# Neighbour rows of layer 0 summed by accumulating gathers, with running sums of ranks in columns beside each row

## The chip, the core and the metric

The kernel runs on one core of one Trainium2 chip. The engines are named as in the profile: PE (TensorE, matrix products), DVE (VectorE), ACT (ScalarE), POOL (GpSimd) and SP (SyncE, which here only issues DMA transfers). POOL issues the indirect transfers: gathers and scatters of rows by a list of indices. The metric is the device time of one execution in microseconds (us).

## What is computed

The reference takes node features `x` (3327 x 512, float32), a sparse random adjacency matrix `adj` (3327 x 3327, integers, about 0.12% ones) and the weights of four graph layers. Each layer adds its result to `x`:

```python
h = maximum(layernorm(x), 0)
# layer 0
mask = (adj > 0); deg = sum(mask, axis=1)
agg = mask @ h / maximum(deg, 1)
out = concat([h @ W_self + b_self, agg @ W_nb + b_nb]) @ W_comb + b_comb
x = x + relu(out)
# layers 1 to 3: graph attention with 8, 4 and 1 heads
e = leaky_relu(f_src[i] + f_dst[j], 0.2), only where adj > 0
x = x + softmax(e) @ (h @ W)      # layer 2 with an elu around the result
```

The result is the `x` after layer 3.

## The kernel before

**Two paths in one program.** `gnn_stack_kernel` holds a fast path, which uses lists of neighbours, and at its end a branch. The one-element tile `flag_i` says whether the fast path was allowed to do what it did; if it is not zero, `general_path` (from L26) computes all four layers again with the dense adjacency matrix and writes the output anew.

```python
    general = nc.values_load(
        flag_i[0:1, 0:1], min_val=0, max_val=1, skip_runtime_bounds_check_because="the result of a comparison"
    )
    with tc.If(general != 0):
        general_path(
```

**Chunks and slots.** Nodes are kept in chunks of 128 (NK = 26 chunks, D = 512 columns). The fast path reads `adj` once, finds the neighbours of each node and sorts the nodes by degree, so that chunk 0 holds the nodes of highest degree. `ROWS` (L564) says how many nodes, at most, have more than 0, 1, 2, ... neighbours: 3328, 3072, 2592, 1984, ... down to 32, 32, 32, 32, 0, 0. From it follows how many neighbour slots a chunk has: 14 for chunk 0, 8 for chunk 1, then fewer, and 1 for chunks 24 and 25, in all 117. SLOTS is 16.

**The first stage** (L852 to L1513) fuses the weights of layer 0, multiplies each chunk by both fused matrices (`pz` for the neighbours' part, `py` for the node's own), stores the neighbours' part into a table in device memory (`table[0]`) and reads `adj`. Then the nodes are sorted: `places` (L1415) works in the tile `work`, 416 columns (W = SLOTS x NK) at a time. Columns 0 to 415 take `run`, the running counts of nodes by degree class, and columns 416 to 831 take `place`; out of these come `rank`, the position of each node, and its integer form. `spread` (L1461) copies the ranks into a tile `rank4` of 4 columns per node, which `store_rank` writes beside each row of `table[0]`, so that a gathered row brings along the position of its node. `scatter` moves each node's record to its sorted position in `own`.

**The flag.** `certain` (L1472) adds up three kinds of doubt: whether the neighbour lists agree with the row's sum of squares, whether a node has more than 16 neighbours, and whether a degree class has more nodes than `ROWS` allows. The last reads `run` at the end of each class, every 26th column from 25, and compares it with `caps`, which holds `ROWS` from its end, so from 0, 0, 32 up to 3328:

```python
                    nc.vector.tensor_tensor(
                        over, box["run"].rearrange("p (d k) -> p d k", k=NK)[:, :, NK - 1], caps, ALU.is_gt
                    )
```

`tell` sums the doubts of all partitions by a matmul (L1492), and `flag` (L1496) makes `flag_i` of whether the sum is above zero.

**Layer 0 and the attentions** (from L1516). `gather` (L1545) issues one indirect transfer per slot, each of up to 128 rows, into the next free places of a ring of 33 rows (`ring`). In layer 0 the index comes from the node's record (`srec`), in layers 1 to 3 from `nbr`, the positions that layer 0 has taken from the gathered rows (L1862). In layer 0, PE adds up the first slots by multiplying with the identity (`sum_on_pe`, L1593), DVE scales that sum by 1/degree and adds the node's own part (L1871) and the bias (L1879), adds the remaining slots, scaled, one by one (L1887), and adds relu of that to x (L1895). `project` (L1602) then normalises the chunk, turns it (L1694), multiplies it with the weights of the next layer (L1780) and stores the rows of the next table. `attend` (L1911) does an attention layer over the same slots.

**The order** is not that of the source. Each stage hands its steps to a `Plan` (L614), with an engine, an estimated cost, a rank and what they wait for. `Plan.run` walks through them by these costs and emits them in the order of their planned starts; each engine then keeps that order. `ORDERS` (L578) gives the order of the chunks by layer, in units of one or two chunks. A layer's first gather waits until all rows of its table are stored (the `mark` at L2194).

**The general path** has no slots. Layer 0 (L136 to L251) projects all chunks, then reads `adj` by chunk, clips it (L213), makes a row code of it (L214), turns it on PE (L223), multiplies the turned mask with the projected rows (L232) and stores the codes (L227, L228, L235 to L237). `attention` (L254) runs once for each of layers 1 to 3: projections of all chunks (L291 to L309), the maximum over each row's neighbours, by head, with one DVE instruction over 1664 columns in layers 1 and 2 and 3328 in layer 3 (L351, after L347 in layer 3), and then, by block of four chunks, head and chunk, the scores and their product with the values:

```python
                                nc.scalar.activation(
                                    t2[:, :w], sb[:, 1, :w], AF.Identity, bias=fd02[:, k, h : h + 1]
                                )
                                nc.vector.scalar_tensor_tensor(
                                    v[:, kk, :w], sb[:, 0, :w], fsd[:, k, d : d + 1], t2[:, :w], ALU.add, ALU.max
                                )
```

These are L419 and L422; L426 adds the mask, L429 takes the exponential, and PE multiplies at L434 (layer 1), L446 (layer 2) or L439 and L442 (layer 3).

Of the kernel before, what the change touches and what calls it, by code (L numbers as in the profile page):

```python
# [8 lines left out]
F32 = mybir.dt.float32  # L9
# [9 lines left out]
P = 128  # L19
# [7 lines left out]
def general_path(  # L27
# [519 lines left out]
    def l3_finish(pc, i, o):  # L547
# [24 lines left out]
ON_DVE = {  # L572
    0: {S: min(S // 2, 5) for S in range(1, SLOTS + 1)},
    1: {S: min(S // 2, 5) for S in range(1, SLOTS + 1)},
    2: {S: 0 for S in range(1, SLOTS + 1)},
}

ORDERS = {  # L578
    0: (
        (24,), (12, 21), (11,), (6,), (18,), (17,), (15,), (4,), (3,), (20,), (5, 9), (22,), (10, 19), (1,),  # L580
        (2,), (14,), (0,), (23,), (8,), (13, 16), (7,), (25,),
    ),
# [110 lines left out]
def gnn_stack_kernel(  # L693
# [32 lines left out]
    heads = {1: l1_w.shape[0], 2: l2_w.shape[0], 3: 1}  # L726
    width = {0: D + 4, 1: D + 8, 2: D + 4, 3: D + 4}
    WIDE = D + 8

# [5 lines left out]
    with ExitStack() as st:  # L735
# [116 lines left out]
        with tc.tile_pool(name="p0", bufs=1) as pa, tc.tile_pool(name="p0p", bufs=2, space=PSUM) as pp:  # L852
# [312 lines left out]
            def empty_rows():  # L1165
                nc.gpsimd.memset(null, 0.0)
                nc.gpsimd.tensor_copy(null[:, 0, D:], null_f[:, 0:1].to_broadcast([P, WIDE - D]))
                nc.gpsimd.memset(null[:, 1, D:], NEVER)
# [128 lines left out]
            for p0 in range(0, NK, 2):  # L1297
# [25 lines left out]
                for j, i in enumerate(unit):  # L1323
# [136 lines left out]
            with nc.allow_non_contiguous_dma(reason="each node's record and place beside its row"):  # L1460
                def spread():  # L1461
                    rank4 = pa.tile([P, NK, 4], F32, tag="rank4", name="rank4")
                    nc.vector.tensor_copy(rank4, box["rank"].unsqueeze(2).to_broadcast([P, NK, 4]))
# [52 lines left out]
        with tc.tile_pool(name="run", bufs=1, reuse_waits="tile") as pr, tc.tile_pool(  # L1516
# [28 lines left out]
            def gather(layer, i, rank, barrier):  # L1545
# [8 lines left out]
                for s in range(S):  # L1554
# [291 lines left out]
            for number, unit in enumerate(ORDERS[0]):  # L1846
                rank = (0, number)
                updated = []
                for j, i in enumerate(unit):
# [14 lines left out]
                    last.append(plan.add("dve", 0.03 + 0.17 * len(runs_of(i, 0, S)), rank, emit, landed))  # L1864
                    left = S - ON_DVE[0][S]
                    summed = sum_on_pe(key, g, list(range(left)), [[o] for o in landed], rank)
                    last += summed

                    def emit(i=i, key=key):
                        acc = tiles["acc", key]  # L1870
# [4 lines left out]
                    done = plan.add("dve", 0.7, rank, emit, [summed[-1], own_in])  # L1875

                    def emit(key=key):
                        acc = tiles["acc", key]
                        nc.vector.tensor_tensor(acc, acc, biasf, ALU.add)  # L1879

                    done = plan.add("dve", 0.7, rank, emit, [done])
                    for s in range(left, S):

                        def emit(i=i, key=key, g=g, s=s):
                            m = held(i, s)
                            acc = tiles["acc", key][:m, :]
# [4 lines left out]
                        done = plan.add("dve", 0.7, rank, emit, [done, landed[s]])  # L1891
                        last.append(done)

# [17 lines left out]
            def attend(layer, number, unit, barrier):  # L1911
# [348 lines left out]
```

## Time and profile before

| what | us |
|---|---|
| median of 14 runs | 1075.08 (1071.61 to 1080.6) |
| the profiled execution | 1075.53 |
| its span, first to last instruction | 1073.6 |

The mean granted clock of PE in this execution was 0.899 of full speed. By stage, busy us of each engine (from a question on five stretches of the span):

| stretch, us | stage | PE | DVE | ACT | POOL | granted clock | DMA share |
|---|---|---|---|---|---|---|---|
| 0 to 266 | adjacency, sorting, first products | 231.78 | 187.30 | 163.20 | 104.96 | 0.96 | 0.87 |
| 266 to 449 | layer 0 | 167.20 | 130.62 | 78.60 | 110.22 | 0.98 | 0.81 |
| 449 to 620 | layer 1 | 143.06 | 144.44 | 103.01 | 129.83 | 0.92 | 0.73 |
| 620 to 870 | layer 2 | 200.23 | 171.52 | 125.76 | 140.46 | 0.82 | 0.53 |
| 870 to 1073 | layer 3 | 134.37 | 91.62 | 47.54 | 135.12 | 0.83 | 0.62 |

How to read the lines that follow. A line of the timeline has the start in us from the span's start, the duration in us, the engine, the line of the source, the operation, what it writes and reads (written as out<-in), the shape, and the count where equal ones are merged; in brackets the idle time before it and what ended that. A line of a group has the same names, the count, and after the bar the busy time in us, the mean duration of one in ns, and the idle time before them. A float32 matmul appears as two PE records where it multiplies, and as one where it turns a tile. "DMA share" is the mean busy share of the core's 16 DMA engines.

### The profile page before, as it was taken

To read this page: it belongs to the slowest core of one execution; us is meant where nothing else is said; L and a number is where in the kernel's file an instruction comes from. 1 tells how busy PE (TensorE), PEld (TensorE's weight loads), DVE (VectorE), ACT (ScalarE), POOL (GpSimd) and SP (SyncE) were. 2 spreads that over 40 slices of the span, in tenths; PEclk is the share of its full clock that TensorE was granted. 3 is DMA by queue.
4 is the path that set the end of the run, shared out by engine and by line. 5 is a ranking of instruction groups with operands and counts; after the bars stand their busy time and mean duration, and the time that the engine had idled before them with its cause. 6 is when DMAs were issued, how large, how long until landed. Compare 5 with 4: busy or idle time off the path is not lost. (4 is left out here: it accounts for less than half of the span.)

```text
span 1073.6 us, 11605 instructions
## 1 busy us (share of the span) xinstructions
PE 876.6 (82%) x2853; PEld 499.2 (46%) x2853; DVE 725.5 (68%) x1848; ACT 518.1 (48%) x1700; POOL 620.6 (58%) x719
## 2 busy tenths in 40 slices
PE   7699999994899998569998983897989814949785
PEld 4244444441476665446665652444544412424332
DVE  6499989920787769278998882787885808435541
ACT  3398887631353534346677641564663612214221
POOL 1051444673777772277787604788777057777671
PEclk9899999997899999879999987798878956979887
DMA  9999888399999986277777604767766147677671
GB/s 350 313 371 392 308 300 302 125 310 327 298 331 311 339 280 195 92 202 219 235 209 216 186 22 125 203 192 204 219 184 173 57 126 190 200 206 208 189 200 54
DMA packets 89910, 240.49 MB, mean 224 GB/s; under 512 B 24933, under 2 KB 26477, under 8 KB 89834
## 3 DMA queue, kind: packets, MB, share of 16 engines
q0 software_dynamic: 41600, 137.72, 43.9%
q1 hardware_dynamic: 48234, 101.96, 26.8%
q8 instruction: 24, 0.39, 0.1%
q14 instruction: 52, 0.43, 0.1%
HBM read 190.35 MB, written 49.27 MB: 223 GB/s over the span
## 5 line engine op out<-in xcount | busy, mean ns | idle before, releaser
L1562 POOL DMA_INDIRECT ring<-table,nbr x351 | 379.0, 1080 | 117.1 <-issue 64.4
L1593 PE MATMUL acc<-ring,ident 128*128 128x512 f32 (+1 forms) x494 | 257.5, 656 | 71.7 <-DVE ring L2110 46.0
L1780 PE MATMUL pw<-w,hT 128*128 128x264 f32 (+1 forms) x832 | 194.3, 390 | 2.8 <-ACT hT L1705 2.8
L1780 PEld LDWEIGHTS pw<-w,hT 128*128 128x128 f32 x832 | 160.1, 193 | 43.5 <-ACT hT L1705 9.7
L1593 PEld LDWEIGHTS acc<-ring,ident 128*128 128x128 f32 (+1 forms) x494 | 95.6, 208 | 175.8 <-issue 79.0
L1562 POOL DMA_INDIRECT ring<-table,srec x117 | 110.2, 942 | 45.5 <-issue 20.1
L2110 DVE TENSOR_TENSOR ring<-ring,w 128x2048 f32<-128x2048 f32 (+7 forms) x76 | 114.3, 1532 | 1.8
L1941 DVE TENSOR_TENSOR e<-ring,fs 128x24 f32<-128x24 f32 (+25 forms) x96 | 15.3, 172 | 132.7 <-DMA ring<-table,nbr 129.0
L1209 DVE FIND_INDEX8 fidx<-one_i,ai 128x8 uint32<-128x832 int32 x104 | 104.2, 1018 | 0.0
L2060 PE MATMUL pw<-w,hT 128*128 128x512 f32 x208 | 98.9, 620 | 5.8 <-ACT hT L2052 5.8
L1217 ACT ACTIVATE junk<-ai 128x1664 int8<-128x1664 int32 (+1 forms) x52 | 82.8, 1591 | 30.1 <-DMA ai<-in_adj_dram 29.6
L1349 PE MATMUL pz_n<-wf,hT_n 128*128 128x512 f32 x208 | 92.3, 595 | 0.9 <-ACT hT_n L1342 0.8
L1349 PE MATMUL py_n<-wf,hT_n 128*128 128x512 f32 x208 | 91.9, 592 | 0.0
L1705 ACT ACTIVATE hT<-pt 128x128 f32<-128x128 f32 (+1 forms) x312 | 81.7, 292 | 21.1 <-PE pt L1694 20.7
L2060 PEld LDWEIGHTS pw<-w,hT 128*128 128x128 f32 x208 | 41.1, 201 | 61.8 <-issue 46.8
L1705 ACT ACTIVATION_READ_ACCUMULATOR hT<-pt 128x1 f32 x312 | 69.4, 223 | 0.0
L822 ACT ACTIVATE ln<-mv,eps 128x1 f32<-128x1 f32 (+1 forms) x60 | 18.0, 300 | 96.2 <-DVE mv L1650 87.7
L1968 ACT ACTIVATE ex<-el 128x48 f32<-128x48 f32 (+19 forms) x56 | 12.8, 232 | 104.3 <-DVE el L1951 104.3
L1349 PEld LDWEIGHTS pz_n<-wf,hT_n 128*128 128x128 f32 x208 | 39.0, 190 | 50.5 <-issue 45.2
L2046 PE MATMUL pt<-ident,y 128*128 128x128 f32 x96 | 15.6, 294 | 56.4 <-DVE y L2030 51.0
L2194 POOL MEMSET mark<- 1x1 f32 x3 | 0.3, 88 | 106.0 <-DMA table<-t 106.0
L2030 DVE SCALAR_TENSOR_TENSOR acc<-ring,w,acc 128x512 f32<-128x512 f32 (+2 forms) x67 | 50.5, 754 | 13.6 <-ACT acc L2028 12.0
(185 smaller groups left out, 1321.8 us busy)
## 6 DMA issues: line engine op xcount, KB each, us to landing
ai<-in_adj_dram SPq DMA_DIRECT2D x25, 832.0 KB, 7.2
ai<-in_adj_dram SPq DMA_DIRECT2D x25, 831.5 KB, 7.3
table<-t SPq DMA_DIRECT2D x52, 258.0 KB, 3.4
xy<-own SPq DMA_DIRECT2D x26, 512.0 KB, 5.6
table<-t SPq DMA_DIRECT2D x26, 260.0 KB, 5.4
table<-zt_n SPq DMA_DIRECT2D x26, 256.0 KB, 5.9
ring<-table,nbr POOLq DMA_INDIRECT x351, 3.8
later<-in_x_dram SPq DMA_DIRECT2D x15, 256.0 KB, 6.7
```

What stands on the lines that cost most here:

```text
L822: nc.scalar.activation(ln, var, AF.Ln, bias=eps, scale=scale)
L1209: nc.vector.max_index(fidx[:, i, qq * 8 : (qq + 1) * 8], one_i, ai[:, q * QW : min(cols, (q + 1) * QW)])
L1217: nc.scalar.activation(junk[:, :cols], tiles["ai", key][:, :cols], AF.Square, accum_out=sq[:, i, hf : hf + 1])
L1349: nc.tensor.matmul(pz, tiles["hT", key][:, c, :], wf[s][:, c, :], start=(c == 0), stop=(c == DC - 1))
L1562: nc.gpsimd.indirect_dma_start(out=ring[:m, r0 + s, : width[layer]], out_offset=None, in_=table[layer], in_offset=bass.IndirectOffsetOnAxi ...
L1593: nc.tensor.matmul(acc, ident[:m, :], g[:m, s, :D], start=(k == 0), stop=(k == len(slots) - 1))
L1705: nc.scalar.activation(hT[:, c, :n], pt[:, c, :n], AF.Copy, accum_out=hsum[layer][:, i, c : c + 1])
L1780: nc.tensor.matmul(pw[:, b, :w], tiles["hT", key][:, c, :], wsb[layer][:, c, b, :w], start=(c == 0), stop=(c == DC - 1),)
L2030: nc.vector.scalar_tensor_tensor(to[:m, :], row, weight, acc[:m, :], ALU.mult, ALU.add)
L2046: nc.tensor.transpose(pt[:, c, :], tiles["y", key][:, c * P : (c + 1) * P], ident)
L2060: nc.tensor.matmul(pw[:, 0, :], tiles["hT", key][:, c, :], w3[:, c, :], start=False, stop=(c == DC - 1))
L2110: nc.vector.tensor_tensor(v, v, box["w"][:m, j, lo:hi, :].unsqueeze(3).to_broadcast([m, hi - lo, H, O]), ALU.mult,)
```

## The change

In layer 0 each chunk now takes one row of the ring instead of one per slot. The first slot is gathered into it, and every further slot is gathered on top with an adding transfer. The ranks move ahead of the row and take 16 columns instead of 4; a chunk with S slots gathers slot s from column 16 - S + s on, so that rank column 16 - S + s takes the ranks of slots 0 to s. The positions are then the first of these columns and the differences of neighbouring ones. ACT scales the sum by 1/degree into PSUM, and DVE adds the own part and the bias. The copy of the ranks goes into columns of the tile `work` instead of a tile of its own. The order of chunks in layer 0 is another, and `AHEAD` sets how much earlier than its chunk each slot's transfer is ranked.

```diff
 ON_DVE = {
-    0: {S: min(S // 2, 5) for S in range(1, SLOTS + 1)},
...
+AHEAD = 0.9
...
     0: (
-        (24,), (12, 21), (11,), (6,), (18,), (17,), (15,), (4,), (3,), (20,), (5, 9), (22,), (10, 19), (1,),
-        (2,), (14,), (0,), (23,), (8,), (13, 16), (7,), (25,),
+        (23,), (22,), (17, 18), (21,), (24,), (9,), (13,), (19,), (11,), (3,), (16,), (5,), (4,), (12,), (6, 20), (2,),
+        (14,), (8,), (15,), (7,), (10,), (1,), (0,), (25,),
...
-    width = {0: D + 4, 1: D + 8, 2: D + 4, 3: D + 4}
-    WIDE = D + 8
+    width = {0: D + SLOTS, 1: D + 8, 2: D + 4, 3: D + 4}
+    WIDE = D + SLOTS
...
-                nc.gpsimd.tensor_copy(null[:, 0, D:], null_f[:, 0:1].to_broadcast([P, WIDE - D]))
+                nc.gpsimd.tensor_copy(null[:, 0, :SLOTS], null_f[:, 0:1].to_broadcast([P, SLOTS]))
...
-                        nc.sync.dma_start(table[0][i * P : (i + 1) * P, :D], tiles["zt", key])
+                        nc.sync.dma_start(table[0][i * P : (i + 1) * P, SLOTS:], tiles["zt", key])
...
                 def spread():
-                    rank4 = pa.tile([P, NK, 4], F32, tag="rank4", name="rank4")
-                    nc.vector.tensor_copy(rank4, box["rank"].unsqueeze(2).to_broadcast([P, NK, 4]))
-                    box["rank4"] = rank4
+                    ranks = box["work"][:, : NK * SLOTS].rearrange("p (k s) -> p k s", s=SLOTS)
+                    nc.vector.tensor_copy(ranks, box["rank"].unsqueeze(2).to_broadcast([P, NK, SLOTS]))
+                    box["ranks"] = ranks
 
                 def store_rank():
-                    nc.sync.dma_start(table[0][:NP, :].rearrange("(k p) w -> p k w", p=P)[:, :, D:], box["rank4"])
+                    nc.sync.dma_start(table[0][:NP, :].rearrange("(k p) w -> p k w", p=P)[:, :, :SLOTS], box["ranks"])
...
+            def add_up(i, rank):
+
+                S = slots_of[i]
+                slot = ring_at[0]
+                ring_at[0] += 1
+                row = ring[:, slot, :]
+                landed = None
+                for s in range(S):
+
+                    def emit(s=s):
+                        m = held(i, s)
+                        lo = SLOTS - S + s
+                        how = {"compute_op": ALU.add} if s else {}
+                        nc.gpsimd.indirect_dma_start(
+                            out=row[:m, lo:],
+                            out_offset=None,
+                            in_=table[0],
+                            in_offset=bass.IndirectOffsetOnAxis(ap=srec[:m, i, s : s + 1], axis=0),
+                            element_offset=lo,
+                            **how,
+                        )
+
+                    turn = (rank[0], rank[1] - AHEAD * (S - 1 - s))
+                    issue = plan.add("pool", pool_cost(held(i, s)), turn, emit, [landed] if landed else [])
+                    landed = plan.add("dma", 0.8 * held(i, s) / P, rank, None, [issue], lag=2.5)
+                last = []
+                ring_readers[slot] = last
+                return row, landed, last
...
-                    g, landed, last = gather(0, i, rank, [])
+                    g, landed, last = add_up(i, rank)
...
-                        for lo, hi, m in runs_of(i, 0, S):
-                            nc.vector.tensor_copy(nbr[:m, base_of[i] + lo : base_of[i] + hi], g[:m, lo:hi, D])
...
-                    left = S - ON_DVE[0][S]
-                    summed = sum_on_pe(key, g, list(range(left)), [[o] for o in landed], rank)
...
-                        nc.vector.scalar_tensor_tensor(
-                            acc, acc, rdeg[:, i : i + 1], tiles["xy", key][:, D:], ALU.mult, ALU.add
-                        )
...
-                        nc.vector.tensor_tensor(acc, acc, biasf, ALU.add)
...
-                            nc.vector.scalar_tensor_tensor(
-                                acc, g[:m, s, :D], rdeg[:m, i : i + 1], acc, ALU.mult, ALU.add
+                        at = base_of[i]
+                        nc.vector.tensor_copy(nbr[:, at : at + 1], g[:, SLOTS - S : SLOTS - S + 1])
+                        if S > 1:
+                            nc.vector.tensor_tensor(
+                                nbr[:, at + 1 : at + S], g[:, SLOTS - S + 1 : SLOTS], g[:, SLOTS - S : SLOTS - 1], ALU.subtract
+                            )
...
+                        nc.scalar.activation(new("acc", key, [P, D], pp), g[:, SLOTS:], AF.Copy, scale=rdeg[:, i : i + 1])
...
+                    for what in ("y", "bias"):
...
+                            nc.vector.tensor_tensor(
+                                acc, acc, biasf if what == "bias" else tiles["xy", key][:, D:], ALU.add
+                            )
...
+            ring_at[0] = 0
             for layer in (1, 2, 3):
```

More of the change, by code (lines that the diff above doesn't have):

```diff
@@ L1864, in gnn_stack_kernel @@
-                    last.append(plan.add("dve", 0.03 + 0.17 * len(runs_of(i, 0, S)), rank, emit, landed))
-                    left = S - ON_DVE[0][S]
-                    summed = sum_on_pe(key, g, list(range(left)), [[o] for o in landed], rank)
-                    last += summed
-                    def emit(i=i, key=key):
-                        acc = tiles["acc", key]
-                        nc.vector.scalar_tensor_tensor(
-                            acc, acc, rdeg[:, i : i + 1], tiles["xy", key][:, D:], ALU.mult, ALU.add
-                        )
@@ L1875, in gnn_stack_kernel @@
-                    done = plan.add("dve", 0.7, rank, emit, [summed[-1], own_in])
-                    def emit(key=key):
-                        acc = tiles["acc", key]
-                        nc.vector.tensor_tensor(acc, acc, biasf, ALU.add)
[L1881 to L1886, printed above, removed]
-                            nc.vector.scalar_tensor_tensor(
-                                acc, g[:m, s, :D], rdeg[:m, i : i + 1], acc, ALU.mult, ALU.add
-                            )
-                        done = plan.add("dve", 0.7, rank, emit, [done, landed[s]])
-                        last.append(done)
+                        at = base_of[i]
@@ new lines, in emit @@
+                        nc.vector.tensor_copy(nbr[:, at : at + 1], g[:, SLOTS - S : SLOTS - S + 1])
+                        if S > 1:
+                            nc.vector.tensor_tensor(
+                                nbr[:, at + 1 : at + S], g[:, SLOTS - S + 1 : SLOTS], g[:, SLOTS - S : SLOTS - 1], ALU.subtract
+                            )
+                    last.append(plan.add("dve", 0.35, rank, emit, [landed]))
+                    def emit(i=i, key=key, g=g):
+                        nc.scalar.activation(new("acc", key, [P, D], pp), g[:, SLOTS:], AF.Copy, scale=rdeg[:, i : i + 1])
@@ new lines, in gnn_stack_kernel, with emit @@
+                    done = plan.add("act", 0.75, rank, emit, [landed], take=("acc",))
+                    last.append(done)
+                    for what in ("y", "bias"):
+                        def emit(key=key, what=what):
+                            acc = tiles["acc", key]
+                            nc.vector.tensor_tensor(
+                                acc, acc, biasf if what == "bias" else tiles["xy", key][:, D:], ALU.add
+                            )
+                        done = plan.add("dve", 0.7, rank, emit, [done, own_in])
```

## The prediction

> **What bounds the kernel now.** I read the page first, then the order in time on the vector engine (DVE) where the flag is made, then layer 0: its stretch of POOL in time and its DMA view. The page's head:
>
> ```profile
> span 1073.6 us, 11605 instructions
> ```
>
> The profiled execution took 1075.53 us, 1.9 us outside its span and 0.45 us above the median of the runs, 1075.08. All of it is the fast path: the last things in the chain of work that ended last are the loading of `flag_i` (L2212, 0.51 us) and one output scatter. So the flag is zero, and nothing of `general_path` runs. How the flag comes about, on DVE in order of time (start, duration, engine, line):
>
> ```profile
> 213.51 0.99 DVE L1419 TENSOR_TENSOR_SCAN ai_sort<-ai_sort,pm_tot 128x416 f32<-128x416 f32 x1
> ...
> 217.14 0.21 DVE L1463 COPY rank<-rank 128x104 f32<-128x104 f32 x1
> ...
> 221.26 0.17 DVE L1482 TENSOR_TENSOR over<-ai_sort,caps 128x16 f32<-128x16 f32 x1
> ...
> 253.74 0.14 DVE L1499 CAST flag_i<-flag_f 1x1 int32<-1x1 f32 x1
> ```
>
> To be seen: the running counts are written at 213.51, the ranks are spread at 217.14 into a tile of their own, and the counts are read again at 221.26, after the spread.
>
> In layer 0 POOL issues its 117 gathers every 1.25 us without a pause, 265.9 to 411, and the DMA engines are 93% taken meanwhile (two queues: packets, MB, share; then the gathers, us to landing):
>
> ```profile
> q0 software_dynamic: 8713, 28.47, 60.9%
> q1 hardware_dynamic: 5908, 16.58, 32.4%
> ...
> ring<-table,srec POOLq DMA_INDIRECT x117, 5.3
> ```
>
> The last gather starts at 410.53, layer 1's first at 449.19:
>
> ```profile
> 410.53 0.95 POOL L1562 DMA_INDIRECT ring<-table,srec  x1 [0.30 <-issue]
> 444.76 0.09 POOL L2194 MEMSET mark<- 1x1 f32 x1 [33.28 <-DMA table<-t]
> 449.19 0.95 POOL L1562 DMA_INDIRECT ring<-table,nbr  x1 [4.35 <-DMA table<-t]
> ```
>
> So layer 0 is POOL's pace, then a tail of 33 us from the last landing (near 416), in which PE works off 34 of 38 us.
>
> **The decisive part: what `spread` writes over.** After the change `spread` writes NK x SLOTS = 416 columns of `work`, from column 0. `run`, the running counts, is `work[:, :W]` with W = 416: the same columns. `certain` still reads `run` at 16 places (25, 51, ... of the 416) and asks whether each is above `caps`. In the instruction order of both kernels the spread stands before this read, with 15 DVE instructions between, as the trace shows at 217.14 and 221.26. So `over` compares ranks. Place 25 is now the rank of a node of chunk 25 // 16 = 1; `caps[0]` is the last of ROWS, 0. The ranks are a permutation of 0 to 3326, so of the 128 nodes of chunk 1 at least 127 have a rank above 0. `okay` is positive, `flag_i` is 1, and after its four layers the program branches into `general_path` and computes everything again with dense adjacency. The output is still what the reference asks; the time is the sum of both paths. I argue this from the code; no trace of before can show it.
>
> **The fast path after the change.** The 117 issues stay: 146 us at 1.25. An accumulating gather must wait for the landing of the one before it in its row. In the new order on POOL most stand 4 to 8 places behind that one (15 of 91 at 4, 19 at 5, 28 at 6, 10 at 7), but the last six stand 3, 3, 3, 2, 2 and 1 behind. Walking the 117 in that order, start = the later of 1.25 us after the one before and that landing: with every landing 3.9 us after its issue (median of all gathers) the last lands at 153, with 5.3 (layer 0's) at 161, with 6.5 at 178, with 7.9 (the longest gather in the trace) at 205; before it was 145 + 5 = 150. How long an accumulating gather takes no row shows. Bounds: a plain one's 3.9, and twice the engine time. That time is 60.9% of 145 us for 14,144 rows, 0.80 us per 128 rows; 10,816 rows accumulate, so doubling adds 67 us to 135. I take 6.5, nearest to layer 0's own median: +28. The Trainium skill, "Collectives: The Full Stack", "Why ReduceScatter is half of AllGather", says that an adding DMA reads two sources on the same ring and so runs at half the rate; that speaks against the change, would use the whole +67, and no accumulating row here tests it.
>
> PE loses 67 sums of L1593 (58 us at 0.86, if PE set the pace) and DVE 50 adds and 34 casts; POOL's 1.25 us hides both until 411, so only the tail gains: ACT copy 0.7, three DVE adds 2.1, statistics 0.9, ACT and DVE refinement 1.2, relu 0.8, turn 0.6, hT 2.1, projection 3.7, copies 0.9, store 3.4, some 18 hand-offs at 0.1 to 0.3, in all 20 to 24 against 33. That gives -11. The wider table rows, 64 B instead of 16 B of ranks, and the wider copy at L1464 (0.6 us by the 416-column rows) lie under the scatter. Fast path: 1075.5 + 28 - 11 = 1092; bounds 1065 (landing 3.9: +3, tail of 20: -13) and 1166 (issues of twice 0.95: 146 + 86 + 8 = 240 against 150, no gain at the tail).
>
> **The general path, by rows of the trace.** It has 26 chunks and, per attention, 7 blocks (six of four chunks, one of two). Prices, first by form (busy, mean ns), then in time:
>
> ```profile
> L2110 DVE TENSOR_TENSOR ring<-ring,w 128x2048 f32<-128x2048 f32 x25 | 57.1, 2289 | 1.3
> L2030 DVE SCALAR_TENSOR_TENSOR acc<-ring,w,acc 128x512 f32<-128x512 f32 x56 | 42.3, 755 | 13.3 <-ACT acc L2028 12.0
> L2110 DVE TENSOR_TENSOR ring<-ring,w 128x1536 f32<-128x1536 f32 x12 | 21.0, 1753 | 0.3
> ```
>
> ```profile
> 150.92 3.60 PE L1349 MATMUL py_n<-wf,hT_n 128*128 128x512 f32 x8
> ...
> 411.68 3.72 PE L1780 MATMUL pw<-w,hT 128*128 128x264 f32 x16
> ...
> 1051.29 3.12 DVE L2030 SCALAR_TENSOR_TENSOR acc<-ring,w,acc 128x512 f32<-128x512 f32 x4 [0.76 <-ACT acc L2028]
> ```
>
> The eight PE records are four instructions, at (3.60 - 0.59) / 7 = 0.43 each record: 0.86 us per 128x512 f32 matmul. The sixteen give 0.222, so 0.445 per 128x264. A turn is 0.11 (eight in 1.04). The four DVE records hang on each other: (3.12 - 0.755) / 3 = 0.79 a step. A step that does not hang on the last one starts some 0.08 before that ends (L1895 runs 0.69 from 342.89, L1862 starts at 343.50): 0.67 a step. L2110's two forms give 1.047 ns an element: 1.89 us for 1664.
>
> 1. Preparation and projections, L139 to L190: PE 248 x 0.86 + 136 x 0.11 = 228; with loading and the 26 statistics 250.
> 2. Adjacency, L195 to L248: PE per chunk 26 x (0.86 + 0.11) = 25.2, above DVE's 18 and ACT's 11; x26 + a start of 15 = 670.
> 3. Projections of three attentions, L275 to L311: 26 x (4 x 0.11 + 4 x 0.86 + 4 x 0.2 + 0.11) = 125, statistics 26 x 0.87 = 23, weights 22; 170 x 3 = 510.
> 4. Row maxima, L321 to L380, on DVE: 624 x (1.89 + 0.10 for the read of the accumulator, ACT's 0.19 less the overlap) = 1242; layer 3: 26 x (3.63 + 0.10 + 3.63) = 191; refilling `fdb`, 22 MB at the 350 GB/s of the page's best slices, 63; turns and round trips 45. 1541. The Trainium skill, "VectorE: DVE Perf Modes", "The perf-mode tier table", has one-source bf16 operations four times as fast as one element a cycle, which would make L347 about 1.0 instead of 3.63, 68 us less; no row shows such an operation in that mode.
> 5. Scores, L387 to L470. Layers 1 and 2 are DVE's: 52 steps (L422 and L426) per head and block, two independent ones in turn, so 0.70, between 0.67 and 0.79; a half block's step 0.43. 72 x 52 x 0.70 + 12 x 52 x 0.43 = 2889; ACT, 2 x 0.69 + 1.06 per 4 DVE steps of 2.8, stays under it. Ends of the blocks 185 (312 short adds at 0.2 to 0.24; per chunk a reciprocal of 0.2 and two or four 512-wide steps of 0.69). Layer 3 is PE's: 1352 x 0.445 = 602, blocks' ends 50. 3726.
>
> Sum 6697. These PE prices are at a granted clock of 1.0; the profile's mean is 0.90, and items 1, 2, 3 and 5 hold 1861 us of PE work: +0 to +207, I take +60. The 91 loops over a head and block hand on at their ends: 0 to 3 us each, I take 1: +91. General path 6848, and with 1092 it is **7940 us**.
>
> Ends: DVE steps at 0.67 (-112), clock 1.0 (-60), no hand-offs (-91), L347 fast (-68), accumulator reads hidden (-62), fast path at 1065 (-27), stages 1 and 3 overlapping (up to -110): 7410, say 7400. Steps at 0.79 (+337), clock 0.9 (+147), hand-offs of 3 us (+182), reads at 0.22 (+75), fast path at 1166 (+74): 8755, say 8800.
>
> **The rivals.** *The flag stays zero, and not slower* (0.02): `certain` sees intact counts, or the branch is not taken, and accumulating gathers land like plain ones. For it: the flag is zero now. Against it: the same columns, the order on one engine. Then only the fast path counts: 1075.5 + 3 - 13 = 1065. It decides with one comparison, whether `over` is positive anywhere; from a landing of 5.3 us down the gathers cost no more than the tail gains. *The flag stays zero, and the adding DMA costs double* (0.01): 135 + 67 us of DMA time and a landing of 5 are 207 against 150, so 1075.5 + 57 - 11, near 1120. *The flag is one, and the row maxima run at two cycles an element* (0.07): L351 is a form that the trace lacks; 624 x 1.89 + 26 x 3.63 = 1274 more, 9200. *The flag is one, and the scores keep step with the hanging DVE pace* (part of the forecast's high side): 8300 to 8800.
>
> **How the numbers follow.** The flag raised: 0.97, of which 0.07 is the two-cycle case and some 0.08 lies outside the sum's other ends. So 7400 to 8800 holds about 8 in 10. A measurement of this kernel can tell about 0.2%, 2 us, from no change: faster 0.015, same 0.005, slower 0.98.
>
> **What would show it.** Right: a span above 7000 us; L419, L422, L426 and L351 among the costliest groups; L422 and L426 near 2366 records each at about 0.75 us; PE well below half busy; the fast path's output scatters ending near 1090 us. Each step can be read by itself: stage 4 from L351's mean (1.9 against 3.6), stage 5 from the start-to-start time of L422 and L426, stage 2 from PE's share there. Wrong: a span near 1.1 ms with no line below L560.

## The result: 7310.02 us, 6.80 times the kernel before

The changed kernel takes 7310.02 us (median of 10 runs, 7299.67 to 7313.43), the kernel before beside it 1075.44 us (47 runs): ratio 6.795, 95% interval 6.783 to 6.808. The profiled execution took 7315.36 us. The mechanism is the predicted one, a raised flag and both paths in one run; the time lies below the range, so terms of the sum were mis-sized.

The head of the page after, with the busy time of each engine (share of the span, instructions):

```profile
span 7313.3 us, 59282 instructions
## 1 busy us (share of the span) xinstructions
PE 4845.6 (66%) x18655; PEld 2708.4 (37%) x18655; DVE 5553.3 (76%) x9677; ACT 3566.1 (49%) x5905; POOL 755.3 (10%) x867
```

There were 11,605 instructions before and there are 59,282 now: another program runs after the first. Why it runs is to be read on DVE in order of time, at the place where the spread ranks and the flag are made:

```profile
216.98 0.37 DVE L1464 COPY ai_sort<-rank 128x416 f32<-128x416 f32 x1
...
221.26 0.17 DVE L1483 TENSOR_TENSOR over<-ai_sort,caps 128x16 f32<-128x16 f32 x1
```

Both rows name the same tile: the spread of the ranks (L1464) writes 416 columns of the tile in which the running counts stood, and 4.3 us later L1483 compares that tile with `caps`. In the kernel before the spread (L1463 there) went into a tile of its own.

The same execution by stages: the stretch, its length, the busy time of PE, weight loads, DVE, ACT and POOL, then granted clock, DMA share and GB/s.

```profile
265.00:506.00 241.00, 138.01 (x520) 106.49 (x520) 95.24 (x280) 95.98 (x389) 164.35 (x118) 0.79 0.91 205
506.00:1117.00 611.00, 475.36 (x1560) 271.52 (x1560) 407.42 (x1023) 276.63 (x1078) 403.99 (x379) 0.86 0.63 178
1117.00:1382.00 265.00, 235.07 (x632) 110.71 (x632) 63.32 (x128) 39.89 (x62) 2.14 (x8) 0.95 0.13 44
1382.00:2032.00 650.00, 631.20 (x2028) 296.38 (x2028) 318.82 (x446) 248.62 (x313) 60.64 (x105) 0.99 0.42 147
2032.00:2202.00 170.00, 132.99 (x549) 76.40 (x550) 56.14 (x154) 35.22 (x53) 0.97 (x2) 0.90 0.05 10
2202.00:3014.00 812.00, 30.40 (x129) 21.20 (x127) 762.94 (x863) 0.75 (x2) 0.58 (x2) 0.52 0.15 48
3014.00:4834.00 1820.00, 1342.11 (x3120) 360.08 (x3120) 1814.35 (x3228) 1600.46 (x2241) 0.28 (x1) 0.98 0.07 21
...
5430.00:6397.00 967.00, 713.19 (x5424) 646.83 (x5424) 962.08 (x1714) 814.91 (x1112) 0.14 (x1) 0.96 0.07 23
...
6712.00:7313.00 601.00, 588.73 (x2704) 513.84 (x2704) 274.76 (x489) 205.31 (x268) 14.64 (x27) 0.99 0.08 28
```

The first two rows are layer 0 and layers 1 to 3 of the fast path; at 1117 the general path begins. Its stages follow: preparation, adjacency, layer 1's projection, row maxima (DVE 763 of 812 us), scores (DVE 1814 of 1820), then layer 2's scores (DVE 962 of 967) and layer 3's (PE 589 of 601). So the bounds were named rightly: DVE in the scores of layers 1 and 2, PE in layer 3's.

Layer 0 of the fast path took 183.3 us before (from its first gather to layer 1's first) and takes 241.2 now. Its last gathers on POOL (start, duration, the wait before it), and the two DMA queues between 265 and 483 (q0 with the gathers, q1 with the other transfers; packets, MB, share of 16 engines) with the median time to landing:

```profile
462.59 1.54 POOL L1588 DMA_INDIRECT ring<-table,srec  x1 [0.30 <-issue]
464.44 1.35 POOL L1588 DMA_INDIRECT ring<-table,srec  x1 [0.31 <-issue]
467.75 1.43 POOL L1588 DMA_INDIRECT ring<-table,srec  x1 [1.95 <-DMA ring<-table,srec]
...
481.62 1.34 POOL L1588 DMA_INDIRECT ring<-table,srec  x1 [3.63 <-DMA ring<-table,srec]
502.21 0.09 POOL L2216 MEMSET mark<- 1x1 f32 x1 [19.25 <-issue]
506.63 1.00 POOL L1563 DMA_INDIRECT ring<-table,nbr  x1 [4.34 <-DMA table<-t]
```

```profile
q0 software_dynamic: 14304, 29.11, 73.5%
q1 hardware_dynamic: 6681, 18.87, 25.2%
...
ring<-table,srec POOLq DMA_INDIRECT x117, 6.4
```

A gather now occupies POOL for 1.54 us and the next starts 1.84 after it; before it was 0.95 and 1.25. Near the end POOL waits for the landing of the row's gather before. The DMA engines, 93% taken before, are 99% taken. From the last gather to layer 1's first it is 25.0 us, before 38.7.

The scores, where half of the new time is spent, on DVE in order of time (the duration covers both instructions of an "x2"), and the groups that carry this and the maxima (busy us, mean ns, idle before):

```profile
3501.66 1.43 DVE L422 SCALAR_TENSOR_TENSOR v<-sb,fsd,t 128x512 f32<-128x512 f32 x2
3502.98 1.31 DVE L426 SCALAR_TENSOR_TENSOR v<-mk,v 128x512 f32<-128x512 int8 x2
3504.19 1.43 DVE L422 SCALAR_TENSOR_TENSOR v<-sb,fsd,t 128x512 f32<-128x512 f32 x2
```

```profile
L422 DVE SCALAR_TENSOR_TENSOR v<-sb,fsd,t 128x512 f32<-128x512 f32 x2028 | 1431.2, 748 | 305.0 <-PE acc L442 240.5 <-ACT t L419 43.1 <-issue 21.5
L426 DVE SCALAR_TENSOR_TENSOR v<-mk,v 128x512 f32<-128x512 int8 x2028 | 1308.8, 687 | 0.0
L351 DVE CUSTOM_DVE_ANT_0 jk<-rc,fdb 128x1664 bf16<-128x1664 bf16 x624 | 1132.1, 1887 | 54.9 <-DMA rc<-rc 43.1 <-DMA fdb<-fdT 11.4
...
L351 DVE DVE_READ_ACCUMULATOR2_ANT dmx<- 128x1 f32 x650 | 53.6, 83 | 0.0
```

From 3501.66 to 3504.19 are 2.53 us for four steps, 0.633 a step. L426 costs 687 ns and L422 748.

### The profile page after: what moved, and what is told of

Same layout as the page of the kernel before. It is cut to its first block, busy times and chain, and to the rows that moved or that the text cites. A ratio compares the mean times of both kernels' runs of the same rounds, so it can differ in the third digit from the quotient of the medians.

```text
span 7313.3 us, 59282 instructions
## 1 busy us (share of the span) xinstructions
PE 4845.6 (66%) x18655; PEld 2708.4 (37%) x18655; DVE 5553.3 (76%) x9677; ACT 3566.1 (49%) x5905; POOL 755.3 (10%) x867
## 3 DMA queue, kind: packets, MB, share of 16 engines
q1 hardware_dynamic: 131986, 330.13, 13.7%
## 5 line engine op out<-in xcount | busy, mean ns | idle before, releaser
L419 ACT ACTIVATE t<-sb,fd 128x512 f32<-128x512 f32 (+1 forms) x2366 | 1508.2, 680 | 1728.8 <-DMA sb<-s 1189.8
L422 DVE SCALAR_TENSOR_TENSOR v<-sb,fsd,t 128x512 f32<-128x512 f32 (+1 forms) x2366 | 1578.8, 709 | 333.9 <-PE acc L442 264.3
L434 PE MATMUL accT<-v,wh 128*65 128x512 f32 (+1 forms) x2912 | 1337.6, 580 | 478.0 <-ACT v L429 457.6
L426 DVE SCALAR_TENSOR_TENSOR v<-mk,v 128x512 f32<-128x512 int8 (+1 forms) x2366 | 1436.0, 649 | 0.1
L429 ACT ACTIVATE v<-v 128x1024 f32<-128x1024 f32 (+1 forms) x1183 | 1176.2, 994 | 265.4 <-DVE v L426 258.1
L351 DVE CUSTOM_DVE_ANT_0 jk<-rc,fdb 128x1664 bf16<-128x1664 bf16 x624 | 1132.1, 1887 | 54.9 <-DMA rc<-rc 43.1
L446 PE MATMUL acc<-wh,v 128*128 128x129 f32 x5408 | 709.4, 285 | 257.4 <-ACT v L429 257.2
L434 PEld LDWEIGHTS accT<-v,wh 128*65 128x65 f32 x2912 | 342.9, 138 | 1431.2 <-ACT v L429 1063.8
L446 PEld LDWEIGHTS acc<-wh,v 128*128 128x128 f32 x5408 | 643.8, 195 | 323.1 <-ACT v L429 322.9
L232 PE MATMUL acc<-z,m 128*128 128x512 f32 x1352 | 592.1, 597 | 10.4 <-ACT m L226 10.4
L442 PE MATMUL acc<-wh,v 128*128 128x257 f32 x1352 | 405.2, 381 | 0.0
L439 PEld LDWEIGHTS acc<-wh,v 128*128 128x128 f32 x1352 | 256.0, 189 | 57.9 <-ACT v L429 19.8
L442 PEld LDWEIGHTS acc<-wh,v 128*128 128x128 f32 x1352 | 257.8, 191 | 36.4
```

The source lines that it names most:

```text
L232: nc.tensor.matmul(acc, m[:, k, :], z[:, k0 + k, :], start=(k0 + k == 0), stop=(k0 + k == NK - 1))
L351: nc.vector.tensor_tensor_reduce(jk, rc, fdb[:, h, :], 1.0, -4.0 * BIG, ALU.add, ALU.max, dmx[:, q, i, h : h + 1],)
L419: nc.scalar.activation(t2[:, :w], sb[:, 1, :w], AF.Identity, bias=fd02[:, k, h : h + 1])
L422: nc.vector.scalar_tensor_tensor(v[:, kk, :w], sb[:, 0, :w], fsd[:, k, d : d + 1], t2[:, :w], ALU.add, ALU.max)
L426: nc.vector.scalar_tensor_tensor(vv, mk[:, :nb, k, :], BIG, vv, ALU.mult, ALU.add)
L429: nc.scalar.activation(v[:, :, :w], v[:, :, :w], AF.Exp)
```

## The experiments

The first four kernels (e1 to e4) ran on a chip on which the kernel before took 1236.46 us (1225.46 to 1250.83, 17 runs), 15% more than in the prediction, so their times are only set against that. The trace of e2, whose first part is the kernel before, shows where: layer 0 lasts 246.9 us against 183.3, and there are stretches (the hold-ups, below) in which DVE, ACT and PE start little while POOL gathers on. On ACT in layer 1:

```profile
558.44 0.81 ACT L1678 ACTIVATE h<-xres,nmr,rs 128x512 f32<-128x512 f32 x1 [1.75 <-DVE nmr L836]
577.35 0.58 ACT L1805 COPY t<-pw 128x512 f32<-128x512 f32 x1 [18.10 <-remote]
```

The last projection that L1805 could wait for had ended on PE near 555. In the profiled run of the prediction the same copy follows the ACTIVATE without a wait. What holds the engines up was not found. Three of the four kernels were therefore run again on other chips.

**e1, the ranks in columns of their own.** Only the place of the spread is changed:

```
-ranks = box["work"][:, : NK * SLOTS].rearrange(...)
+ranks = box["work"][:, 2 * W : 3 * W].rearrange(...)
```

> The kernel after, but spread copies the ranks into columns 832 to 1247 of work instead of 0 to 415. My theory (the ranks overwrite the running counts, so the flag is raised and general_path runs): only the fast path is left. In the profile after, the last output scatter starts at 1116.5 us against 1061.4 before, 55 later, so 1075.5 + 55 = 1131 us, no line below L560, layer 0 as in the profile after (accumulating gathers of 1.54 us on POOL, layer 1's first gather 506.6). Rival (the flag is raised for another reason, such as sums that come out wrong or a doubt in the lists): still near 7310 us. What I forecast for the fast path was 1092, with 1065 to 1166 as its bounds.

1227.24 us, ratio to the kernel before 0.995 (0.991 to 0.998). The general path is gone, so the overwritten counts alone raise the flag. The expected 5% did not show here: with the hold-ups layer 0 takes 239.5 us, against 246.9 in the kernel before.

**e7, the same kernel on a chip without the hold-ups** (before 1074.12 us).

> The same kernel as e1 (ranks in columns of their own, nothing else changed), because the chip of e1 ran the kernel before at 1236 us and its trace has stretches of some 20 us in layers 0 to 2 in which ACT, DVE and PE start almost nothing while POOL goes on gathering; the profiled run of the prediction has none. Theory (the adding gather's own pace, 1.84 us against 1.25, costs layer 0 some 57 us wherever POOL is what paces layer 0): on a chip that runs the kernel before at about 1075 us, 1125 to 1135 us, ratio 1.047 to 1.055, layer 1's first gather at about 507 us. Rival (the adding gathers cost nothing, and the 55 us of the changed kernel's fast part have to do with the raised flag): ratio 0.99 to 1.00 there too. On a chip that again runs the kernel before at about 1236 us both expect 0.995.

1127.84 us, ratio 1.0498 (1.0461 to 1.0535): the theory's. From layer 0's first gather to the start of the last (the walk, below) it is 212.2 us, before 144.6; from there to layer 1's first 26.5, before 38.7.

**e2, the kernel before with the overwrite alone.** One copy more, behind the spread:

```
+over_run = box["work"][:, : NK * SLOTS].rearrange("p (k s) -> p k s", s=SLOTS)
+nc.vector.tensor_copy(over_run, box["rank"].unsqueeze(2).to_broadcast([P, NK, SLOTS]))
```

> The kernel before, with one more DVE copy in spread: the ranks, 16 times, over columns 0 to 415 of work, as the change does it; all else as before, plain gathers included. My theory: that copy alone brings the general path, whose share after is about 7315 - 1131 = 6184 us, so 1075.5 + 6184 = 7260 us. Rival (the accumulating gathers or the new table layout raise the flag): 1075.5 us, no change.

7409.25 us (one run), 6173 above the kernel before on that chip. The changed kernel's own share is 7310.02 - 1127.84 = 6182. One DVE copy of 0.4 us that costs 6.2 ms: the overwrite is enough, and nothing else of the change is needed for it.

**e3, gathers that don't add.**

```
-how = {"compute_op": ALU.add} if s else {}
+how = {}
```

> As e1_own_columns, but the gathers do not add: each slot's row overwrites the one before (the sum of neighbours is left out; the ranks are taken directly instead of as differences). Same order, same waits, same number of gathers. My theory (the adding itself costs: 0.59 us more on POOL per gather and about twice the time of the DMA engines): POOL back to 1.25 us a gather, landing near 5.3, so the gathers end near 161 us after the first against 216, and the time is 1131 - 55 = 1076, within 1065 to 1085. Rival (the chain of waits in one row and the new order cost the 55 us, not the adding): still 1120 or more.

1272.4 us, ratio 1.030 (1.022 to 1.037), slower than e1: a miss. The walk did shorten, to 149.8 us, but 139.1 us passed after it until layer 1, in which PE caught up with projections that had stood still in stretches like the one above (PE was busy for 19 us of the first 152).

**e8, the same kernel without the hold-ups** (same chip as e7).

> The same kernel as e3 (ranks in their own columns, gathers overwrite instead of adding, so that only the last neighbour's row is counted). Theory: layer 0's walk takes 150 us as in e3, since every gather is issued at 1.25 us; where ACT, DVE and PE are not held up, the kernel ends at 1060 to 1080 us on a chip that runs the kernel before at 1075, ratio 0.985 to 1.005, and the tail after the last landing is 20 to 25 us. Rival (short walk or long, the layer lasts until PE has done the projections, as in e3, where 138 us passed after the last issue): 1100 us or more, ratio over 1.02.

1072.53 us, ratio 0.998 (0.997 to 1.000), 55.3 us below e7. Layer 0's gathers of both, e7's first (busy us, mean ns, idle before):

```profile
L1588 POOL DMA_INDIRECT ring<-table,srec x117 | 164.2, 1403 | 59.6 <-issue 29.6 <-DMA ring<-table,srec 19.8 <-DVE rdeg L1507 10.2
```

```profile
L1588 POOL DMA_INDIRECT ring<-table,srec x117 | 110.1, 941 | 65.1 <-issue 29.3 <-DMA ring<-table,srec 26.0 <-DVE rdeg L1507 9.8
```

The same 117 gathers of the same rows keep POOL busy 54 us longer when 91 of them add. The waits for landings, 20 and 26 us (with the usual 0.3 of each), are there in both, so they don't need the adding. They go with the chain within a row and with busy DMA engines: in e3, with the same chain, the other transfers took 9.2% of the engines during the walk, against 31.5% here, and the waits were 3.9 us. So the walk is 164.6 us here and not 150 as in e3. The adding also raises the gathers' time on the DMA engines. The queues during the walk, e7's (265 to 479) and then e8's (265 to 431):

```profile
q0 software_dynamic: 14304, 29.11, 72.9%
q1 hardware_dynamic: 6729, 19.07, 25.5%
```

```profile
q0 software_dynamic: 8912, 29.11, 55.3%
q1 hardware_dynamic: 6714, 19.00, 31.5%
```

For the same 29.11 MB the gathers take 72.9% of 214 us, 156, against 55.3% of 166, 92: per 128 rows 0.83 us plain and 1.59 us added, 1.9 times as much.

**e4 and e12, half of the adding bytes.** The adding gathers bring the ranks and 256 of the 512 columns:

```
-out=row[:m, lo:],
+out=row[:m, lo : SLOTS + D // 2] if s else row[:m, lo:],
```

> As e1_own_columns, but the adding gathers take only the ranks and the first 256 of the 512 columns (half of the neighbours' sum is left out). It tells POOL's issue from the DMA engines' time, which both fill layer 0 after the change (117 issues: 26 x 1.27 + 91 x 1.84 = 200 of 216 us; DMA share 98.8%). Theory POOL (descriptors per row are written one by one, whatever their length): an adding gather still takes about 1.54 us on POOL, only the waits of some 16 us go, 1131 - 10 = 1121, between 1115 and 1131. Theory DMA (the engines' time sets the pace and holds POOL up): their time falls by about a third, POOL's instruction shortens with it, 1085 to 1100.

On the chip of e1: 1222.99 us, ratio 0.989 (0.983 to 0.995), 4 us from e1. Run again:

> The same kernel as e4 (ranks in their own columns; adding gathers bring the ranks and 256 of the 512 columns, the other 256 columns' sums are left out), on a chip without the hold-ups of e4's. Theory (POOL's 1.54 us per adding issue sets layer 0's pace): the issues stay at 1.54 us, the walk shortens only by what POOL waited for landings, 8 to 16 us: ratio 1.034 to 1.045. Rival (the DMA engines set the pace): half of the adding bytes gone, the walk back to about 150 us, ratio 0.99 to 1.01.

1113.12 us, ratio 1.034 (1.032 to 1.037), as the theory had it. Its gathers on POOL, and the two queues during its walk (267 to 471):

```profile
L1588 POOL DMA_INDIRECT ring<-table,srec x117 | 164.1, 1403 | 50.0 <-issue 34.1 <-DVE rdeg L1507 10.0 <-DMA ring<-table,srec 5.9
```

```profile
q0 software_dynamic: 14304, 18.07, 53.6%
q1 hardware_dynamic: 6706, 18.97, 27.5%
```

The gathering queue moves 18.07 MB instead of 29.11 and takes 53.6% of the DMA engines instead of 72.9%, and POOL is busy for the same time within 0.1 us. What shrinks is the wait for landings, 5.9 us against 19.8; the ratio's gain of 0.0155 is 17 us, 11.6 of them in layer 0 (227.1 against 238.7). So an adding gather's 1.54 us on POOL don't depend on its bytes, and with DMA engines that are 81% taken such issues still leave the kernel 37 us above the one before. What the engines alone would cost, if POOL issued every 1.25 us, no run shows: they are 98% taken over e7's 214 us, 211 us of work, against 87% of 166, 144, in e8, so by this estimate they could hold the gathers nearly as long as POOL does. So relieving one of the two limits would bring little while the other stands.

**e5, one operand's form.** The changed kernel with the mask step's constant in a column:

```
-vv, mk[:, :nb, k, :], BIG, vv, ALU.mult, ALU.add
+vv, mk[:, :nb, k, :], big_c[:, 0:1], vv, ALU.mult, ALU.add
```

> The changed kernel with one operand of the mask step (L426 of the scores) taken from a column of memory instead of an immediate number. Theory (the form of the scalar sets the cost: 755 ns with a column, 690 with an immediate, as the rows of the kernel before have it): L426's mean rises by about 65 ns, which over 1872 steps that DVE paces in layers 1 and 2 is 120 us: about 7430 us. Rival (the 8-bit mask operand makes the step cheaper than an all-float one): the mean stays where it is and so does the time, 7310 us.

7443.11 us (one run), 133 above the changed kernel. The two lines, by form, two numbers lower in the source (L428 is the former L426):

```profile
L428 DVE SCALAR_TENSOR_TENSOR v<-mk,big_c,v 128x512 f32<-128x512 int8 x2028 | 1431.6, 748 | 0.0
L424 DVE SCALAR_TENSOR_TENSOR v<-sb,fsd,t 128x512 f32<-128x512 f32 x2028 | 1431.1, 748 | 296.1 <-PE acc L444 232.3 <-ACT t L421 42.9 <-issue 20.9
```

687 has become 748: the step costs what L422 costs, so the 8-bit mask makes nothing cheaper and the immediate constant does. And 1872 full steps of layers 1 and 2 by 0.061 are 114 us, the half blocks' 312 by 0.065 another 20: the end moved by all of it, so DVE paces these scores throughout.

**e6, more of layer 0's sums on DVE, in the kernel before.**

```
-0: {S: min(S // 2, 5) for S in range(1, SLOTS + 1)},
+0: {S: min((S + 1) // 2, 6) if S > 1 else 0 for S in range(1, SLOTS + 1)},
```

> The kernel before with 12 of its 494 rank sums of layer 0 moved from PE to DVE (one more per chunk, up to six). Theory: PE is busy for 34 of the 38 us between the last gather's issue and the end of layer 0, and 12 sums of 0.66 us fewer shorten the layer by 5 to 8 us: ratio 0.993 to 0.995. Rival (the tail is the projections of chunks that landed last, which no sum delays): ratio 0.998 to 1.003.

1069.84 us, ratio 0.9964 (0.9943 to 0.9984): faster than the kernel before by 0.4%, and in neither band. (The 494 of the expectation are the PE records of L1593 in all layers; in layer 0 there are 134, two for each of PE's 67 sums.) But layer 0 took 181.7 us, 1.6 less than before, and layer 1, in which nothing was edited, 202.8 against 207.3. **e11** went on, to 73 such steps on DVE (50 before, 62 in e6):

```
+0: {S: min((S + 2) // 2, S - 1) for S in range(1, SLOTS + 1)},
```

> The kernel before with still more of layer 0's rank sums on DVE: all but half of a chunk's neighbours, rounded down and one taken off, at least one left to PE. If the 0.4% that 12 moved sums gained comes from PE's backlog at the end of layer 0, these gain more: ratio 0.988 to 0.994, layer 0 shorter by 6 to 12 us. If it comes from anything else (layer 0 lasted 182 us against 183 there), 0.995 to 1.005.

1074.85 us, ratio 0.9998 (0.998 to 1.0015); layer 0 took 183.1 us. So PE's backlog is not what e6 gained from, and what it gained from stays open.

**e9, the new order of chunks with plain gathers.** The kernel before with the changed kernel's list for layer 0.

> The kernel before with the changed kernel's order of chunks in layer 0 and nothing else of the change. Theory (the order is made for adding gathers; with plain ones POOL's 117 issues at 1.25 us and the tail of PE stay): within 1% of the kernel before, 0.99 to 1.01. Rival (the 55 us of the changed kernel's layer 0 come in good part from the order, which lets the same chunk's rows land late): ratio over 1.02.

1107.03 us, ratio 1.028 (1.025 to 1.031): the rival's number. On POOL, the last gather, the end of layer 0's stores and layer 1's first gather:

```profile
414.87 0.95 POOL L1562 DMA_INDIRECT ring<-table,srec  x1 [0.30 <-DVE acc L1887]
466.75 0.09 POOL L2194 MEMSET mark<- 1x1 f32 x1 [50.92 <-DMA table<-t]
473.46 0.96 POOL L1562 DMA_INDIRECT ring<-table,nbr  x1 [6.63 <-DMA table<-t]
```

The walk is unchanged at 144.7 us, but 58.6 us follow it instead of 38.7. The order puts a chunk with 8 neighbours and one with 14 just before the last, and with plain gathers more of their sums on PE are then still to be made: 13.7 us of L1593 after the last gather against 6.7 in the kernel before, with 9.2 us in which PE waits for ACT's `h` behind them. Layer 0 is 20 us longer in all; the other 11 us lie before and after it, and no run explains them. **e13** asks whether the order costs in the changed kernel too: e1's kernel with the list of before.

> The changed kernel with ranks in their own columns, adding gathers, and layer 0's chunks in the order of the kernel before. e9 showed that the new order alone costs 30 us with plain gathers. Theory (there the order cost because PE's sums of deep chunks came last; with adding gathers PE has no such sums, and the 55 us are POOL's issue time and its waits): by a walk of the gathers at 1.84 and 1.27 us, landing 6.4, the last lands 4 us earlier than in e7, so 1118 to 1130 us, ratio 1.040 to 1.052. Rival (the order costs 20 to 30 us with adding gathers too, so that these cost only the rest): ratio 1.015 to 1.030.

1132.80 us, ratio 1.053 (1.050 to 1.056), not faster than e7's 1.050. So with adding gathers the new order costs nothing, and the 55 us are the gathers'. The walk shortened by 1.9 us, not 4, for the last gather waits 5.46 us for the landing before it; and 33.4 us follow it, against 26.5 in e7:

```profile
477.15 1.54 POOL L1588 DMA_INDIRECT ring<-table,srec  x1 [5.46 <-DMA ring<-table,srec]
506.06 0.09 POOL L2216 MEMSET mark<- 1x1 f32 x1 [27.37 <-DMA table<-t]
510.53 0.99 POOL L1563 DMA_INDIRECT ring<-table,nbr  x1 [4.38 <-DMA table<-t]
```

**e10, a chunk's adding gathers spread further apart** (e1's kernel with AHEAD 2.0 instead of 0.9).

> e1's kernel with the adding gathers of a chunk spread further ahead of it on POOL (AHEAD 2.0 instead of 0.9). Theory (POOL loses 16 us in layer 0 waiting for landings, the rest of the 55 us is its own issue time): by a walk of the 117 gathers at 1.84 and 1.27 us, landing 6.4, the last lands 6 us earlier than in e1; ratio to before 1.040 to 1.048 against e1's 1.050. Rival (the DMA engines, 99% taken in layer 0, set the pace and any order gives the same): 1.048 to 1.053.

1122.87 us, ratio 1.0434 (1.0407 to 1.0462), inside the theory's band but not for its reason alone: the walk shortened by 10.4 us to 201.8, yet layer 1's first gather came at 505.4, as in e7 (504.5), since 37.1 us followed the last issue, against 26.5. That agrees with the rival's full DMA engines, without showing that they set the end: their share over layer 0 is 0.90 in e10 and in e7, 215 us of work in both, whenever POOL issues it. The 5 us appear in the later layers, and why is open.

## Why the prediction was right, and where it was wrong

**Right: the flag.** That the spread covers the counts, that `certain` then compares ranks, and that the branch is taken, all argued from the code, is what the two rows with one tile name show, and e1 and e2 show it from both sides: without the overlap no general path, with the overlap alone all of it. Both rivals with a zero flag fall, though the price that the second named for the adding gathers, near 1120 us, is about what e7 measured: its added DMA time came (156 us in e7 against 92 in e8), beside a price on POOL that it did not have. The rival with maxima at two cycles an element falls with L351's 1887 ns; the one at the hanging pace of 0.79 falls with 0.633. One of the signs did not come: PE was to be well below half busy and was 66% busy. The prediction had priced no PE work in the scores of layers 1 and 2; L434 and L446 keep PE busy for 2047 us there, which lie under DVE's steps.

**Wrong: sizes.** The predicted sum was 1092 + 6848 = 7940; the profiled execution is 1117 + 6196 and 2 us outside the span, 7315. The steps in the prediction's order:

- *Fast path 1092 (1065 to 1166).* 1127.84 by itself (e7), 36 above; in the changed kernel it had its last 11 us beside the general path's start. The tail was right (-12 in e7 for -11), the landing too (6.4 in the changed kernel and 6.9 in e7 for the 6.5 taken). The step that failed is "the 117 issues stay: 146 us at 1.25". An adding gather is issued every 1.84 us, 91 x 0.59 = 54 us more. That price stood only in the upper bound, as twice 0.95. With 14 us of waits for landings (for the 28) and the tail this is 54 + 14 - 12 = 56, e7's layer 0 being 55.4 longer. The rule of the Trainium skill, "Collectives: The Full Stack", "Why ReduceScatter is half of AllGather", stated there for the add of a ReduceScatter, agrees with the queue's own time: 73.5% of 218 us are 160, less 26 plain gathers at 0.80 leaves 1.65 us per 128 added rows, twice 0.80. So the +67 us of engine time, which the prediction named and left out of its sum, came as well (64 between e8 and e7). The rule speaks of the DMA engines, though, and not of POOL, whose price leaves 37 us in e12, with the engines 81% taken; what the engines would cost by themselves stays open.
- *Stages 1 to 3.* 265, 650 and 526 (the three projections, 170 + 186 + 170) for 250, 670 and 510: together 11 above.
- *Stage 4, the maxima.* 812 + 410 + 145 = 1367 for 1541. L351 itself was right at 1887 for 1.89 us. The read of the accumulator is a record of 83 ns that partly overlaps: DVE was busy 763 + 386 = 1149 us in layers 1 and 2 for the 1242 priced, and refills and turns left it idle for 73, with layer 3's 17 for 90, where 108 were priced. In layer 3 L347 runs in 1018 ns where the nearest row gave 3.63 us, 68 us less; the prediction's sentence on the Trainium skill, "VectorE: DVE Perf Modes", "The perf-mode tier table", had about 1.0, and the measurement bears it out for this form:

```profile
L351 DVE CUSTOM_DVE_ANT_0 jk<-r,fdb 128x3328 bf16<-128x3328 bf16 x26 | 93.2, 3617 | 0.1
L347 DVE TENSOR_SCALAR r<-rc 128x3328 bf16<-128x3328 bf16 x26 | 25.5, 1018 | 11.5 <-DMA rc<-rc 11.5
```

- *Stage 5, the scores: the largest miss.* 1820 + 967 + 601 = 3388 for 3726. The step that failed is "two independent ones in turn, so 0.70, between 0.67 and 0.79". It priced both steps by L2030's 755 ns, a step with its scalar in a column. L422 has that form; L426 takes an immediate, and for it the same profile of before had rows of 690 ns, L1895's among them (0.69 in the prediction's own example of the overlap):

```profile
L1895 DVE SCALAR_TENSOR_TENSOR xres<-acc,xy 128x512 f32<-128x512 f32 x26 | 18.0, 691 | 1.0 <-DMA ring<-table,srec 0.2
```

(748 + 687) / 2 less an overlap of 0.08 is 0.637, measured 0.633: below the lower end. 3744 x 0.067 = 251 us; layer 3, 601 for 602 + 50, gives 51 more. The rest is about what the half blocks give: their steps took 477 and 416 ns, less the overlap 0.366 for the 0.43 priced, and 624 of these are 40 us by this estimate.
- *The two surcharges*, 60 for the clock and 91 for hand-offs, were not there. The granted clock was 0.99 in the stages that PE bounds (second and last); in the first and the projections it was 0.90 to 0.95, and what that cost is within the 11 us above. In layer 1's scores DVE was idle for 6 of 1820 us, so its 56 hand-offs had next to nothing to take.

With e7's fast path the balance is 36 - 11 + 11 - 174 - 338 - 60 - 91 = -627, and 7940 - 627 = 7313. The range's low end added up each of these gains only as far as its bounds went. Its floor for the score step, 0.67, came from one kind of step where the stage has two, and that alone, with 3744 steps at 0.037, is 139 us, more than the 90 by which the range missed.

## What to carry to other kernels

Before pricing a moved buffer, write down who still reads the place that it moves to, and when: here a copy of 0.4 us into a scratch area raised a flag worth 6.2 ms. Price each instruction by a row of its own operand form, an immediate and a column of scalars apart, because thousands of steps multiply the difference. Where work is given to a gather that adds, price its issue time on POOL and its time on the DMA engines, both, because here the two lie close together; and set an order of chunks anew for the engine that does the sums.

## What the runs showed of the hardware

An indirect gather that adds occupies POOL for 1.54 us against 0.95, whether it brings 512 columns or 256 (mean of all 117: 1403 ns in both), and takes 1.65 us of the DMA engines' time per 128 rows of 512 columns against 0.80. A scalar_tensor_tensor over 512 f32 columns takes 748 ns with its scalar in a column and 687 with an immediate, the 8-bit second operand changing nothing. And one chip of several ran the layers of the same kernel some 160 us longer in all, with engines held up for up to 18 us beside running gathers, while its general path took as long as elsewhere (6173 and 6182 us); no run here shows why.
